# Two-layer graph network, head products: weights made stationary, two pairs of graphs moving in one product, and the transposed sums turned back by block moves

## Chip, cores and metric

One NeuronCore of a Trainium2 chip runs the kernel, in float32 throughout. The metric is device time in microseconds (us) of one launch, the median of several runs; lower is better. The engines are named as in the profile: PE (TensorE matmul), PEld (its weight load), DVE (VectorE), ACT (ScalarE), POOL (GpSimd) and SP (SyncE, which here issues every DMA; its queue is written SPq).

## The reference

Inputs are 128 graphs of 128 nodes with 256 features, and their weighted adjacency matrices. Both layers are residual with a layer norm and a relu ahead:

```python
h = relu(layernorm(x));  x = x + (adj @ (h @ w0) + b0)                  # layer 0
h = relu(layernorm(x))                                                  # layer 1, h is "feats"
feat = (h @ fc_w + fc_b) -> 8 heads of 256
q = feat @ q_w + q_b;  k = feat @ k_w + k_b                             # one number a node and head
attn = softmax(leaky_relu(q + k.T + (1 - adj) * -1e9, 0.01))            # 8 heads of 128 x 128 a graph
x = x + sigmoid((attn @ feat over heads) @ fp_w + fp_b + h)
```

The kernel multiplies attention by h first, and by one 256 x 256 matrix a head afterwards (fc_w of the head times fp_w of the head, made once in the setup).

## The kernel before

The work is done in 32 groups of 4 graphs (`GB = 4`), in a software pipeline that is written out by hand: `manual_schedule` keeps every engine's instructions in the program's order. While the head products of group g run, the attention of group g+1, the second norm of g+2, and the first layer of g+3 are worked on, and g+4 is loaded.

**The head products.** For each graph the 128 x 256 features h2 are split into two halves of 128 features, and the two graphs of a pair (b = 0, 1) with the two halves (c = 0, 1) make a 2 x 2 block matrix. It is multiplied with the head's 2 x 2 blocks of weights by a scheme of seven products instead of eight (`wt[0]` to `wt[6]`, sums of the weights' blocks made in `setup_sums`; `f[0]` to `f[6]`, sums of the aggregated features made in `take`). A unit is one pair of graphs and one half of the 8 heads, so a group has 4 units. In `aggregate` (L592) the features are stationary and the turned attention of 4 heads (512 columns) moves, which gives the transposed aggregated features `g_ps` in PSUM, four a unit. `take` (L608) makes f0 to f6 of them: three ACT copies, two DVE sums that read PSUM, and two POOL differences (f5 in `five`, L603, and f2). In `multiply` (L636) f is stationary and 128 columns of weights move; the products of unit n-1 run while unit n is aggregated, in the order of `ORDER`:

```python
ORDER = [("g", 0, 0), 3, 0, ("g", 1, 1), 1, 4, ("g", 1, 0), 6, 5, ("g", 0, 1), 2]
```

These are 11 slots a unit and 44 a group. Seven sums over 8 heads gather in two PSUM banks (`acc0`, `acc1`), of the form nodes x features. `combine` (L654) adds them on DVE into z, in two steps (after product 4 and after product 2), once for each pair. `residual_a` (L683, POOL) has added the output bias to h2 before, `residual_b` (L687, POOL) adds h2 to z; `sigmoid` (a tanh on ACT), `finish` (DVE) and `store` follow.

**PSUM.** `ps_m` has 6 banks for everything short-lived, `ps_o` one for each of acc0 and acc1.

**The turn of the attention.** Softmax leaves attn as query x key; `aggregate` needs key x query. `move` (L558) exchanges 32 x 32 blocks between partitions with 16 DMAs a pair of graphs (`attnB`), `turn` (L570) turns the inside of the blocks with one DVE stream transpose a graph. h2 takes the same way (`move_h2` L431, 16 DMAs, and `turn_h2_blocks`). All these are issued by SP.

**What sets the order.** `PLAN` (L714) lists steps as (slot, group ahead, function, arguments); `FIRST_PLAN` and `SECOND_PLAN` are for groups 0 and 1. The steps that issue DMAs, in the order in which SP runs them in a group g: slot 3 `move_h2` of g+2 (16), slot 8 `begin` of g+4 (2) and `load_blocks` of g+3 (4), slot 18 the first 8 blocks of `move` for pair 0 of g+1, slot 28 k_mem of `turn_qk` (1) and the other 8 blocks, slot 30 six blocks of pair 1, slot 34 `load_k` (4), ten blocks of pair 1 and `store` of g-1 (1). That is 60 DMAs a group. `turn` stands at slot 34 for both graphs of pair 0 (for the group to come), and at slots 12 and 13 of the group itself for the two graphs of pair 1, whose first use is the aggregation at slot 22.

At slot 3 ACT's `take(0, 1, 1)` is followed by `n2_apply` of g+2, which writes the h2 that `move_h2` moves; ahead of it on ACT stands `leaky` of the first graph (slot 0), which waits for DVE's `masked` (slot 0: `spread`, a stream transpose, L508, and the mask's sum, L516).

Of the kernel before, what the change touches and what calls it, by code (L numbers as in the profile page):

```python
# [15 lines left out]
P = 128  # L16
# [12 lines left out]
def gnn_then_gat_kernel(  # L29
# [33 lines left out]
    ps_m = ctx.enter_context(tc.tile_pool(name="ps_m", bufs=6, space=PSUM))  # L63
    ps_o = ctx.enter_context(tc.tile_pool(name="ps_o", bufs=1, space=PSUM))
# [24 lines left out]
    fpb_j = const.tile([P, D], FP, name="fpb_j")  # L89

# [11 lines left out]
    sp = setup.enter_context(tc.tile_pool(name="setup", bufs=1))  # L110
    turning = ExitStack()
    tp_ = turning.enter_context(tc.tile_pool(name="turning", bufs=1, side="right"))
    NK = HD // P
    ROWS = NK + 2 * NC
# [4 lines left out]
    nc.sync.dma_start(rows_in[NK + NC : ROWS], k_w.rearrange("(c p) o -> c (p o)", p=P))  # L119
# [6 lines left out]
    def more_loads():  # L126
        nc.sync.dma_start(fpw, fp_w.rearrange("(k p) o -> p k o", p=P))
        nc.sync.dma_start(qkb[:, 0:1], q_b.partition_broadcast(P))
        nc.sync.dma_start(qkb[:, 1:2], k_b.partition_broadcast(P))
        for c in range(NC):  # L130
            nc.sync.dma_start(
                fpb_j.rearrange("p (j c q) -> p c j q", c=NC, q=Q)[:, c],
                fp_b.rearrange("(c j q) -> c j q", j=NB, q=Q)[c].partition_broadcast(P),
            )
# [15 lines left out]
    def setup_rows():  # L150

        cp = ps_m.tile([P, ROWS], FP, name="cp", tag="m")
# [3 lines left out]
            qkc[:, :, 0:2], cols[:, NK:ROWS].rearrange("p (two c) -> p c two", two=2)  # L156
# [21 lines left out]
    def setup_turn(c, both=True):  # L178

        for k4 in range(NK // 4):  # L180
            tp = ps_m.tile([P, 4, P], FP, name="tp", tag="m")
            for kk in range(4):
                nc.tensor.transpose(tp[:, kk, :], fcw[:, c, ts(4 * k4 + kk, P)], ident)
            copy = nc.vector.tensor_copy if both and k4 % 2 else nc.scalar.copy
            copy(
                fcwT[:, ts(k4, 4)].rearrange("p k (j c q) -> p k j c q", c=NC, q=Q)[:, :, :, c],
                tp.rearrange("p k (j q) -> p k j q", q=Q),
            )

    def setup_wqk():  # L190


        wp = ps_m.tile([P, 2, D], FP, name="wp", tag="m")
# [12 lines left out]
    def setup_wqk_turn():  # L206

        tp = ps_m.tile([P, 2, NC, P], FP, name="wt_ps", tag="m")
# [15 lines left out]
    def setup_weights(h, c, on_dve):  # L224

        to = (slice(0, 5, 4), slice(1, 3))
        mp = ps_m.tile([P, D], FP, name="mp", tag="m")
# [11 lines left out]
    def setup_bias():  # L239

        bp = ps_m.tile([P, 1], FP, name="bp", tag="m")
# [28 lines left out]
    def setup_fpb():  # L270

        bp = ps_m.tile([P, D], FP, name="fb_ps", tag="m")
        nc.tensor.matmul(bp, lhsT=ones, rhs=fb, start=True, stop=False)
        nc.tensor.matmul(bp, lhsT=ones, rhs=fb2[:, 0], start=False, stop=True)
        nc.vector.tensor_tensor(
            fpb_j.rearrange("p (j c q) -> p c j q", c=NC, q=Q),
            bp.rearrange("p (c j q) -> p c j q", j=NB, q=Q),
            fpb_j.rearrange("p (j c q) -> p c j q", c=NC, q=Q),
            ALU.add,
        )  # L280
# [81 lines left out]
    def turn_adj(s):  # L362
        tp = ps_m.tile([P, GB, P], FP, name="adj_ps", tag="m")
# [5 lines left out]
    def first_a(s, b2):  # L369
# [3 lines left out]
        pp = ps_m.tile([P, 2, NC, P], FP, name="ah_ps", tag="m")  # L373
# [12 lines left out]
    def first_b(s, b2):  # L386
# [3 lines left out]
        op = ps_m.tile([P, 2, D], FP, name="x1_ps", tag="m")  # L390
# [54 lines left out]
    def turn_h2(s, b2):  # L445
        if b2 == 0:
            s["h2T"] = gp.tile([P, GB, NC, P], FP, name="h2T", tag="h2T", bufs=1)
        tp = ps_m.tile([P, 2, NC, P], FP, name="h2T_ps", tag="m")
# [9 lines left out]
    def make_qk(s, w=wqk):  # L458

        qk = ps_m.tile([P, P], FP, name="qk_ps", tag="m")  # L460
# [12 lines left out]
    def turn_qk(s):  # L473


        tp = ps_m.tile([P, GB, Q], FP, name="q_ps", tag="m")
# [93 lines left out]
    def turn(s, b):  # L570

        aT = s["aT", b] = pool["attnT"].tile([P, H, P], FP, name="attnT", tag="attnT")
        nc.vector.transpose(  # L573
            aT.rearrange("p h (i r) -> p i h r", r=Q), s["ab", b // 2][:, :, b % 2]
        )

    def turn_by_products(s, b):

        aT = s["aT", b] = pool["attnT"].tile([P, H, P], FP, name="attnT", tag="attnT")
        for h4 in range(2):  # L580
            tp = ps_m.tile([P, 4, P], FP, name="aT_ps", tag="m")
            for h in range(4):
                n = H * (b % 2) + 4 * h4 + h
                nc.tensor.transpose(tp[:, h, :], s["a", b // 2][:, ts(n, P)], ident)
            copy = nc.vector.tensor_copy if h4 else nc.scalar.copy
            copy(aT[:, ts(h4, 4)], tp)

    HU = H // 2  # L590

    def aggregate(u, b, c):  # L592
        s, pair, half = u["s"], u["pair"], u["half"]
        u["g", b, c] = ps_m.tile([P, HU, P], FP, name="g_ps", tag="m")
        nc.tensor.matmul(  # L595
            u["g", b, c],
            lhsT=s["h2"][:, 2 * pair + b].rearrange("p j c q -> p (j c q)")[:, ts(c, P)],
            rhs=s["aT", 2 * pair + b][:, ts(half, HU), :],
            start=True,
            stop=True,  # L600
        )

    def five(u):  # L603
        f = u["f"]
        f[5] = pool["un"].tile([P, HU, P], FP, name="f5", tag="f5")
        nc.gpsimd.tensor_tensor(f[5], f[4], f[0], ALU.subtract)  # L606

    def take(u, b, c, with_five=True):  # L608
# [3 lines left out]
        def new(m):  # L612
            f[m] = pool["un"].tile([P, HU, P], FP, name=f"f{m}", tag=f"f{m}")
# [6 lines left out]
        elif (b, c) == (1, 0):  # L620
            nc.vector.tensor_tensor(new(4), g, f[3], ALU.add)  # L621
            nc.vector.tensor_tensor(new(6), f[0], g, ALU.subtract)
            if with_five:
                five(u)
# [7 lines left out]
    ORDER = [("g", 0, 0), 3, 0, ("g", 1, 1), 1, 4, ("g", 1, 0), 6, 5, ("g", 0, 1), 2]  # L632
    FIRST = (3, 6)
    LAST = (4, 2)

    def multiply(u, m):  # L636

        half = u["half"]
        bank, slot = SLOT[m]
        if half == 0 and m in FIRST:  # L640
            u["s"]["acc", u["pair"], bank] = ps_o.tile(
                [P, 4, P], FP, name=f"acc{bank}", tag=f"acc{bank}"
            )
        acc = u["s"]["acc", u["pair"], bank]
        for h in range(HU):
            nc.tensor.matmul(  # L646
                acc[:, slot, :],
                lhsT=u["f"][m][:, h, :],
                rhs=wt[m][:, half * HU + h, :],
                start=(half == 0 and h == 0 and m in FIRST),  # L650
                stop=(half == 1 and h == HU - 1 and m in LAST),
            )

    def combine(u, m):  # L654
# [3 lines left out]
        s, pair = u["s"], u["pair"]  # L658
        z = s["z"][:, ts(pair, 2), :].rearrange("p b (h o) -> p (b h) o", o=P)
# [4 lines left out]
        def both(t):  # L664
            return t.unsqueeze(1).to_broadcast([P, 2, P])

        acc = s["acc", pair, m == 2]
        if m == 4:
            p1 = small.tile([P, P], FP, name="p1", tag="p1", bufs=2)
            w = s["w"] = small.tile([P, 2, P], FP, name="w", tag="w", bufs=2)  # L670
            nc.vector.tensor_copy(p1, acc[:, 0])
            add(w, acc[:, 1:3], both(p1))
            add(z[:, 0], acc[:, 3], p1)
        elif m == 2:
            w = s["w"]
            p6 = small.tile([P, P], FP, name="p6", tag="p6", bufs=2)
            v = small.tile([P, 2, P], FP, name="v", tag="v", bufs=2)
            nc.vector.tensor_copy(p6, acc[:, 0])
            add(v, acc[:, 1:3], both(p6))
            add(z[:, 2:4], w, both(v[:, 0]))  # L680
            add(z[:, 1], w[:, 1], v[:, 1])

    def residual_a(s, pair):  # L683
        h = s["h2"][:, ts(pair, 2)].rearrange("p b j c q -> p b (j c q)")
        nc.gpsimd.tensor_tensor(h, h, fpb_j.unsqueeze(1).to_broadcast([P, 2, D]), ALU.add)  # L685

    def residual_b(s, pair):  # L687
# [16 lines left out]
    def store(s, b0, nb):  # L704
# [22 lines left out]
        (7, "u", take, 0, 1, 0),  # L727
# [6 lines left out]
        (11, -1, residual_b, 1),  # L734
        (11, "u", take, 1, 0, 0),
        (11, 1, leaky, 2),
        (12, 0, turn, 2),
        (12, 1, masked, 3),
        (12, 1, normal, 0),
        (13, 0, turn, 3),  # L740
# [3 lines left out]
        (17, "u", take, 1, 1, 0),  # L744
# [7 lines left out]
        (21, 0, residual_a, 0),  # L752
# [9 lines left out]
        (28, "u", take, 2, 1, 0),  # L762
# [9 lines left out]
        (30, 1, move, 1, range(6)),  # L772
        (31, "u", take, 2, 0, 1),
        (32, "u", combine, 1, 2),
        (32, 0, residual_b, 0),
        (33, "u", take, 3, 0, 0),
        (34, 2, load_k),
        (34, 1, move, 1, range(6, 16)),
        (34, -1, store, 0, GB),
        (34, 1, turn, 0),  # L780
        (34, 1, turn, 1),
# [6 lines left out]
        (39, "u", take, 3, 1, 0),  # L788
# [5 lines left out]
        (43, 0, residual_a, 1),  # L794
# [8 lines left out]
        (7, "u", take, 0, 1, 0, False),  # L803
# [3 lines left out]
        (7, "u", five, 0),  # L807
# [12 lines left out]
        (17, "u", take, 1, 1, 0),  # L820
# [8 lines left out]
        (21, 0, residual_a, 0),  # L829
# [20 lines left out]
        (28, "u", take, 2, 1, 0),  # L850
# [12 lines left out]
        (32, 0, residual_b, 0),  # L863
# [15 lines left out]
        (38, 1, turn, 0),  # L879
        (38, 1, normal, 3),  # L880
        (39, "u", take, 3, 1, 0),
        (39, 3, first_b, 0),
        (39, 3, n2_stats, 0),
        (39, 1, turn, 1),
# [7 lines left out]
        (43, 0, residual_a, 1),  # L892
# [5 lines left out]
    plans = {0: FIRST_PLAN, 1: SECOND_PLAN}  # L898
# [109 lines left out]
    setup_sums(1)  # L1008
    setup.close()
    pool["un"] = ctx.enter_context(tc.tile_pool(name="unit", bufs=2))  # L1010
    units = [None]
    for g in range(NG):
        cur = groups[g]
        cur["z"] = pool["un"].tile([P, GB, D], FP, name="z", tag="z")
        last = units[-1]
        units = [{"s": cur, "pair": i // 2, "half": i % 2, "f": {}} for i in range(4)]
        for slot in range(4 * len(ORDER)):
# [6 lines left out]
            for at_, who, f, *args in plans.get(g, PLAN):  # L1024
                if at_ != slot:
                    continue
                if who == "u":
                    u = last if args[0] < 0 else units[args[0]]
                    if u:
# [76 lines left out]
```

## Time and profile before

| | |
|---|---|
| median of 3 runs | 1513.42 us (1512.85 to 1514.95) |
| profiled execution | span 1512.1 us from first to last instruction, 1.3 us below the median; no other time is recorded for this execution |
| mean granted TensorE clock | 0.996 |
| busy | PE 98%, PEld 79%, DVE 85%, ACT 73%, POOL 66% |
| group period in the middle of the run | 44.89 us (first aggregation of one group to that of the next, the same within 1 ns over groups 2 to 27) |
| first aggregation of groups 0, 1, 2 | at 60.39, 119.36 and 166.78 us |
| first aggregation of groups 28 to 31 | at 1333.86, 1378.81, 1418.46 and 1461.58 us; the last instruction ends at 1512.1 |
| DMAs | 253752 packets, 139.18 MB, the 16 DMA engines 40.5% busy with SP's queue |

A group line of the page reads: line, engine, operation, written<-read tile, shape and count, then busy time and mean duration of one in ns, then the engine's idle time just ahead of it with what ended it. A timeline line reads: start in us, length in us, engine, line, operation, and how many of them are merged. Matmuls are pipelined, so their pace is the distance from start to start and not their duration. A float32 matmul of the program shows as two matmuls. SP has no busy time on the page, since issuing a DMA is not counted as busy: its load is read from the timeline.

### The profile page before, as it was taken

How to read it: one execution, taken by the hardware profiler on the slowest of the kernel's cores; microseconds unless marked ns; L12 is line 12 of the kernel's file. 1: busy time of each engine (PE TensorE's matmuls, PEld its weight loads, DVE VectorE, ACT ScalarE, POOL GpSimd, SP SyncE). 2: the span in 40 equal slices, each digit the busy share in tenths (PEclk: the TensorE clock that was granted, in tenths of full speed). 3: DMA queues.
4: the chain of work that ended last, by engine and by line, in shares of the span. 5: the costliest groups of instructions: out<-in, count | busy, mean ns of one | idle time of the engine just before them, and what ended most of it. 6: DMA issues, size and time to landing. Idle time of an engine off the chain costs nothing.

```text
span 1512.1 us, 30658 instructions
## 1 busy us (share of the span) xinstructions
PE 1478.6 (98%) x9969; PEld 1198.0 (79%) x9969; DVE 1288.5 (85%) x2150; ACT 1103.5 (73%) x3847; POOL 1004.6 (66%) x879
## 2 busy tenths in 40 slices
PE   7889999999999999999999999999999999999998
PEld 5667888887888888888888888888788888888787
DVE  5778988888998888898888898888899888888753
ACT  4888777788777788777778777778877778876641
POOL 5666677676667767667767667767666776766563
PEclk9999999999999999999999999999999999999999
DMA  6124444444434444434444444444443444433320
GB/s 190 31 50 84 98 88 105 92 102 95 97 86 105 97 98 99 97 84 103 108 89 98 95 101 86 106 94 98 96 99 85 106 96 98 97 77 81 73 71 28
DMA packets 253752, 139.18 MB, mean 92 GB/s; under 512 B 169988, under 2 KB 221592, under 8 KB 253336
## 3 DMA queue, kind: packets, MB, share of 16 engines
q1 hardware_dynamic: 253592, 137.23, 40.5%
q8 instruction: 78, 1.28, 0.4%
q14 instruction: 82, 0.67, 0.2%
HBM read 39.60 MB, written 17.30 MB: 38 GB/s over the span
## 4 chain that ended last, share of the span: by engine, by line
PE 91%; DVE 3%; ACT 2%; POOL 1%; SPq 1%; DMA 1%; issue 1%; DVEq 0%; POOLq 0%
PE acc L646 51%; PE g_ps L595 28%; PE x_ps L393 7%; PE ah_ps L377 4%; PE qk_ps L463 1%; ACT attn L545 1%; ACT attn L529 1%; SPq L436 1%; ACT h L329 1%; DVE st L296 0%; DVE attn L508 0%; DVE attn L516 0%; DMA rows_in<-in_L_gnn_k_w_dram 0%; POOL attn L554 0%; DVE nmax L537 0%
## 5 line engine op out<-in xcount | busy, mean ns | idle before, releaser
L646 PEld LDWEIGHTS acc<-wts,f 128*128 128x128 f32 x7168 | 889.0, 192 | 244.7 <-issue 202.0
L646 PE MATMUL acc<-wts,f 128*128 128x128 f32 x7168 | 894.5, 275 | 4.6 <-DVE z L662 2.5
L595 PE MATMUL g_ps<-attnT,h 128*128 128x512 f32 x1024 | 527.1, 597 | 0.0
L545 ACT ACTIVATE attn<-attn,nmax 128x128 f32<-128x128 f32 x1024 | 398.1, 401 | 1.0 <-DVE nmax L537 1.0
L606 POOL TENSOR_TENSOR f<-f,f 128x512 f32<-128x512 f32 x128 | 164.1, 1282 | 268.2 <-DVE f L621 268.2
L529 ACT ACTIVATE attn<-attn,q 128x128 f32<-128x128 f32 x1024 | 313.5, 395 | 18.6 <-DVE attn L516 15.4
L554 POOL TENSOR_TENSOR attn<-attn,total 128x1024 f32<-128x1024 f32 x128 | 245.0, 1914 | 99.0 <-DVE total L553 93.7
L626 ACT COPY f<-g_ps 128x512 f32<-128x512 f32 x128 | 74.0, 578 | 262.4 <-PE g_ps L595 262.4
L545 ACT ACTIVATION_READ_ACCUMULATOR attn<-attn,nmax 128x1 f32 x1024 | 204.8, 200 | 0.0
L627 POOL TENSOR_TENSOR f<-f,f 128x512 f32<-128x512 f32 x128 | 192.4, 1503 | 9.6 <-ACT f L626 6.9
L516 DVE TENSOR_TENSOR attn<-attn,mask 128x1024 f32<-128x1024 f32 x128 | 179.8, 1405 | 4.5
L537 DVE TENSOR_REDUCE nmax<-attn 128x8 f32<-128x1024 f32 x128 | 153.9, 1203 | 17.4 <-ACT attn L529 17.3
L595 PEld LDWEIGHTS g_ps<-attnT,h 128*128 128x128 f32 x1024 | 156.0, 192 | 7.7 <-issue 6.7
L508 DVE STREAM_TRANSPOSE attn<-kq 128x1024 f32<-128x1024 f32 x128 | 157.0, 1227 | 5.3 <-DMA kq<-k_mem 5.3
L573 DVE STREAM_TRANSPOSE attnT<-attnB 128x1024 f32<-128x1024 f32 x124 | 148.6, 1217 | 11.4 <-issue 6.2
L393 PE MATMUL x_ps<-w_sb,ahT 128*128 128x256 f32 x512 | 120.8, 380 | 0.9 <-ACT ahT L384 0.9
L621 DVE TENSOR_TENSOR f<-g_ps,f 128x512 f32<-128x512 f32 x128 | 87.0, 680 | 37.0 <-ACT f L619 32.7
L690 POOL TENSOR_TENSOR z<-z,h 128x256 f32<-128x256 f32 x126 | 89.2, 729 | 34.9 <-DVE z L662 29.8
L685 POOL TENSOR_TENSOR h<-h,fpb_j 128x512 f32<-128x512 f32 x64 | 109.8, 1715 | 0.1
L617 ACT COPY f<-g_ps 128x512 f32<-128x512 f32 x128 | 74.5, 582 | 41.0 <-PE g_ps L595 41.0
L393 PEld LDWEIGHTS x_ps<-w_sb,ahT 128*128 128x128 f32 x512 | 92.7, 191 | 11.8 <-ACT ahT L384 1.8
L700 DVE SCALAR_TENSOR_TENSOR z<-z,x 128x1024 f32<-128x1024 f32 (+2 forms) x34 | 89.2, 2627 | 6.0 <-ACT z L696 6.0
(110 smaller groups left out, 1314.6 us busy)
## 6 DMA issues: line engine op xcount, KB each, us to landing
attnB<-attn SPq DMA_DIRECT2D x992, 64.0 KB, 2.0
xg<-in_x_dram SPq DMA_DIRECT2D x32, 512.0 KB, 4.1
out_dram<-z SPq DMA_DIRECT2D x31, 512.0 KB, 3.1
h2B<-h SPq DMA_DIRECT2D x464, 32.0 KB, 1.9
ag<-in_adj_dram SPq DMA_DIRECT2D x32, 256.0 KB, 4.6
agB<-in_adj_dram SPq DMA_DIRECT2D x116, 64.0 KB, 4.4
fcw<-in_L_gnn_fc_w_dram SPq DMA_DIRECT2D x2, 1024.0 KB, 8.2
fpw<-in_L_gnn_fp_w_dram SPq DMA_DIRECT2D x1, 2048.0 KB, 14.5
```

Source lines behind the costliest of these rows:

```text
L393: nc.tensor.matmul(op[:, bb, :], lhsT=s["ahT"][:, 2 * b2 + bb, c, :], rhs=w0_sb[:, c, :], start=(c == 0), stop=(c == NC - 1),)
L508: nc.vector.transpose(s["v", b], s["kq"][:, :, b].unsqueeze(3).to_broadcast([P, NB, H, Q]),)
L516: nc.vector.tensor_tensor(a, a, s["mask"][:, b, :] .rearrange("p (j c) -> p j c", c=Q) .unsqueeze(2) .to_broadcast([P, NB, H, Q]), ALU.add,)
L529: nc.scalar.activation(a[:, :, h, :], a[:, :, h, :], AF.Prelu, bias=s["q"][:, b, h : h + 1], alpha=0.01,)
L537: nc.vector.tensor_reduce(nmax, a.rearrange("p j h c -> p h j c"), AX.XY, ALU.max, negate=True)
L545: nc.scalar.activation(a[:, :, h, :], a[:, :, h, :], AF.Exp, bias=s["nmax", b][:, h : h + 1], accum_out=s["total", b][:, h : h + 1],)
L554: nc.gpsimd.tensor_tensor(a, a, total.unsqueeze(1).unsqueeze(3).to_broadcast([P, NB, H, Q]), ALU.mult)
L573: nc.vector.transpose(aT.rearrange("p h (i r) -> p i h r", r=Q), s["ab", b // 2][:, :, b % 2])
L595: nc.tensor.matmul(u["g", b, c], lhsT=s["h2"][:, 2 * pair + b].rearrange("p j c q -> p (j c q)")[:, ts(c, P)], rhs=s["aT", 2 * pair + b][: ...
L606: nc.gpsimd.tensor_tensor(f[5], f[4], f[0], ALU.subtract)
L627: nc.gpsimd.tensor_tensor(new(2), f[1], f[5], ALU.subtract)
L646: nc.tensor.matmul(acc[:, slot, :], lhsT=u["f"][m][:, h, :], rhs=wt[m][:, half * HU + h, :], start=(half == 0 and h == 0 and m in FIRST), ...
```

## The change

1. **Products.** `multiply` now takes the weights as stationary operand and moves f. Where a unit held one pair and 4 heads, in groups 2 to 30 it holds both pairs and 2 heads, so 256 columns (two pairs of 128 nodes) move at once, and half as many matmuls are issued. Groups 0, 1 and 31 (`PAIRWISE`) keep one pair a unit and 128 columns. The sums come out transposed, features x nodes, and acc0 and acc1 take two PSUM banks each; `ps_m` goes from 6 to 4 banks (during the setup a second pool `ps_s` lends 2 more).
2. **Summed halves.** `sum_features` (POOL, once a group) adds the two feature halves of every second graph; `aggregate(1, 2)` uses it in the place of (1, 0). `take` copies f4 (ACT), makes f5 on DVE from PSUM and f6 and f2 on POOL; one DVE operation over PSUM a unit goes, one ACT copy comes. `aggregate` issues two matmuls of 256 columns where it issued one of 512.
3. **Attention tiles.** They are kept by pair and half of the heads; `turn` makes both graphs of a pair for 4 heads. In groups 2 to 30 unit 0 needs both pairs' first halves, so `turn(1, 0)` stands at slot 40 of the group before, the second halves at slots 12 and 13.
4. **Way back.** `combine` runs once a group over both pairs and writes `zT`; the output bias is added on ACT (two operations) instead of `residual_a` on POOL. `move_z`, at slot 11, exchanges the blocks of zT with 16 DMAs issued by SP, each 32 partitions of 1 KB; `turn_z`, at slot 20, is one DVE stream transpose; then `residual` on POOL for four graphs. Group 31 turns zT with PE transposes (`turn_z_by_products`).
5. **Setup.** The output bias becomes a column (`fpb_o`), loaded with the other rows.

```diff
-    ps_m = ctx.enter_context(tc.tile_pool(name="ps_m", bufs=6, space=PSUM))
-    ps_o = ctx.enter_context(tc.tile_pool(name="ps_o", bufs=1, space=PSUM))
+    ps_m = ctx.enter_context(tc.tile_pool(name="ps_m", bufs=4, space=PSUM))
...
+    def turn(s, pair, half):
         nc.vector.transpose(
+            attention_tile(s, pair, half).rearrange("p b h (i r) -> p i b h r", r=Q),
+            s["ab", pair][:, :, :, ts(half, HU)],
         )
...
+        for n, pair in enumerate(u["pairs"]):
...
+            nc.tensor.matmul(
+                g[:, n * w : (n + 1) * w],
+                lhsT=lhsT,
+                rhs=s["aT", pair, u["half"]][:, b, u["heads"]],
...
+        elif (b, c) == (1, 2):
+            nc.scalar.copy(new(4), g)
+            nc.vector.tensor_tensor(new(5), g, f[0], ALU.subtract)
+            nc.gpsimd.tensor_tensor(new(6), f[3], f[5], ALU.subtract)
...
             nc.tensor.matmul(
-                acc[:, slot, :],
-                lhsT=u["f"][m][:, h, :],
-                rhs=wt[m][:, half * HU + h, :],
+                acc,
+                lhsT=wt[m][:, u["half"] * HU + h, :],
+                rhs=f[:, n],
...
+    def move_z(s):
+        s["zB"] = pool["un"].tile([P, NB, GB * NC * Q], FP, name="zB", tag="zB", bufs=1)
+        for i in range(NB):
+            for j in range(NB):
+                nc.sync.dma_start(s["zB"][ts(i, Q), j], s["zT"][ts(j, Q), ts(i, D)])
+    def turn_z(s):
+        s["z"] = pool["un"].tile([P, GB, D], FP, name="z", tag="z", bufs=1)
+        nc.vector.transpose(
+            s["z"].rearrange("p (a b) (c j q) -> p j (b c) a q", b=2, j=NB, q=Q),
+            s["zB"].rearrange("p j (k a q) -> p j k a q", a=2, q=Q),
+        )
...
-        (11, -1, residual_b, 1),
+        (11, -1, move_z),
-        (12, 0, turn, 2),
+        (12, 0, turn, 0, 1),
-        (13, 0, turn, 3),
+        (13, 0, turn, 1, 1),
-        (21, 0, residual_a, 0),
+        (20, -1, turn_z),
+        (21, -1, residual, 0),
+        (21, -1, residual, 1),
+        (30, 1, sum_features),
+        (32, 1, move, 1, range(6, 16)),
         (34, 2, load_k),
-        (34, 1, move, 1, range(6, 16)),
-        (34, 1, turn, 0),
-        (34, 1, turn, 1),
+        (34, 1, turn, 0, 0),
+        (40, 1, turn, 1, 0),
-        (43, 0, residual_a, 1),
```

## The prediction

> **What bounds the kernel now.** I read the page first (busy shares and the costliest groups), then the timeline of PE in the middle of the run, then that of SP, which the page gives no share, then those of DVE and ACT at the start of a group.
>
> ```profile
> PE 1478.6 (98%) x9969; PEld 1198.0 (79%) x9969; DVE 1288.5 (85%) x2150; ACT 1103.5 (73%) x3847; POOL 1004.6 (66%) x879
> ...
> attnB<-attn SPq DMA_DIRECT2D x992, 64.0 KB, 2.0
> ...
> h2B<-h SPq DMA_DIRECT2D x464, 32.0 KB, 1.9
> ```
>
> PE has no room: in the middle every group takes 44.89 us, to the ns. Its pace by form is read from start to start (columns: start, length, engine, line, operation, how many):
>
> ```profile
> 701.06 1.89 PE L393 MATMUL x_ps<-w_sb,ahT 128*128 128x256 f32 x8
> 702.79 1.05 PE L646 MATMUL acc<-wts,f 128*128 128x128 f32 x8
> ...
> 706.29 1.95 PE L646 MATMUL acc<-wts,f 128*128 128x128 f32 x16
> 708.08 1.02 PE L595 MATMUL g_ps<-attnT,h 128*128 128x512 f32 x2
> 708.94 1.95 PE L646 MATMUL acc<-wts,f 128*128 128x128 f32 x16
> ```
>
> 128 columns: (708.08-706.29)/16 = 0.112 us a matmul; 256 columns, with a new weight each: (702.79-701.06)/8 = 0.216; 512: 0.86/2 = 0.430. The weight loads hide at all three. So 224 product matmuls x 0.112 + 32 x 0.430 = 38.8 of the 44.9 us.
>
> SP is the other engine that I look at, since the change gives it 16 more DMAs a group. One period of its queue:
>
> ```profile
> 708.17 0.53 SPq L706 DMA_DIRECT2D out_dram<-z  x1
> 712.34 11.49 SPq L436 DMA_DIRECT2D h2B<-h  x16
> 723.95 0.51 SPq L68 DMA_DIRECT2D xg<-in_x_dram  x1
> 724.56 0.45 SPq L70 DMA_DIRECT2D ag<-in_adj_dram  x1
> 725.07 3.15 SPq L78 DMA_DIRECT2D agB<-in_adj_dram  x4
> 729.04 5.00 SPq L565 DMA_DIRECT2D attnB<-attn  x8
> 734.48 0.36 SPq L483 DMA_DIRECT2D k_mem<-k  x1
> 734.88 9.68 SPq L565 DMA_DIRECT2D attnB<-attn  x14
> 744.60 2.04 SPq L488 DMA_DIRECT2D kq<-k_mem  x4
> 746.69 6.21 SPq L565 DMA_DIRECT2D attnB<-attn  x10
> 753.00 0.53 SPq L706 DMA_DIRECT2D out_dram<-z  x1
> ```
>
> The reader is to see that SP is nearly full too. A DMA holds it for about 0.59 us (L565: median 0.589 of 992, minimum 0.507; L436: 0.599), with 0.04 between two, whether it carries 32 or 64 KB. It idles only where data are late: 708.70 to 712.34 (h2 of n2_apply), 728.22 to 729.04 and 734.04 to 734.48, 4.9 us of 44.8. The last blocks of pair 1 are issued at 752.9, 2.6 us into the next group (which starts at 750.32), and land some 1.4 us later; nobody minds, as `turn` of that pair stands at slot 12.
>
> **The change part by part.**
>
> *Products.* In 29 groups 112 matmuls of 0.216 replace 224 of 0.112: 25.09 - 24.19 = 0.90 us. Aggregation: 64 x 0.216 - 32 x 0.430 = +0.06. PE's own work falls by 0.83 us a group, to 44.1; 29 x 0.83 = 24 us if PE stays the bound. The row L393 has the new form, so I take 0.216; by the trace's spread this is not the open question. The Trainium skill (TensorE: Matmul & The Clock Gate, Back-to-back issue gap) gives a warm matmul a fixed 2.5 ns beyond its columns. By that two matmuls saved into one would give back 2.5 ns and not 8, and the sum of this part would be 8 us.
>
> *Sums and their way to z.* DVE: four sums over PSUM of 0.68 go (-2.7 us a group); combine falls from 2 x 2.6 us to about 3.3 to 4.2 (the same columns in half the instructions; rows of 256 columns cost 0.42, of 512 0.68); `turn_z` adds 1.22 (row L573). ACT gets 4 copies of 0.58 and two bias additions of 0.4, +3.1 us (73% to about 80%). POOL loses 2 x 1.72 and gains a sum of about 0.7. None of these is full, so they cost nothing as long as each stays hidden under PE; uncovered, the ACT part would be 3.1 us a group.
>
> *Four banks in the place of six.* From the trace I compared, for each short-lived PSUM tile, its first matmul with the end of the last reader of the tile four before it: the tightest pair has 0.8 us to spare (q_ps behind the third unit's first g_ps), the next 1.9. ACT's added copies can eat this: 0 to 1 us a group. I take 0.
>
> *Setup and end.* Setup changes by tenths of a us, either way. At the end four PE transposes (4 x 0.11 and 0.29 to finish) and two sums of 0.42 enter behind the last sums: +1.3 us.
>
> *16 DMAs on SP.* move_z is partition to partition, 32 rows, as L565 and L436 are; by them it costs 16 x 0.633 = 10.1 us of SP a group. Bounds: the fastest steady row (kq, 0.48 from start to start) gives 7.6, the mean of L436 with its slow ones (0.68) 10.8; nothing in the trace is near zero. I take 10.1, as L565 is nearest. SP works 44.8 - 4.9 = 39.9 us in the period shown and 38.4 in the next, so the 16 make 49 to 50, above PE's 44.1. Here the Trainium skill speaks against me: DMA: Bandwidth & Descriptors (Issuing engines are not separate DMA queues) says that the sequencer's time to start a DMA is usually small beside the DMA itself, and its table for the GpSimd path puts the dispatch at about 50 ns. By that, 16 would cost 0.8 us and the whole would end near 1491. The row of this case, 0.589 of 992, decides.
>
> *What queues behind it.* SP runs in order, so h2B, attnB and z share one line, and its end has become a deadline: `turn(1, 0)` at slot 40 needs all 16 blocks of pair 1 before PE can start the next group. So a loop closes. Call the end of turn(1, 0) T:
>
> - T to the first h2B. DVE goes on with the sum L400, norm statistics, spread and mask, then ACT with leaky, take and n2_apply; only then may SP go on. In the trace of before the same steps, back to back, go from 747.88 (L400 starts) to 757.23 (h2B starts): 9.35 us.
>
> ```profile
> 752.31 2.45 ACT L529 ACTIVATE attn<-attn,q 128x128 f32<-128x128 f32 x8 [0.29 <-DMA attnB<-attn]
> 754.67 0.56 ACT L619 COPY f<-g_ps 128x512 f32<-128x512 f32 x1
> 755.13 2.07 ACT L329 ACTIVATE h<-x,nb,rstd 128x256 f32<-128x256 f32 x4
> ```
>
> - SP without a pause: h2B to agB 15.1 (15.9 and 14.3 in two periods), z 10.1, eight attnB 5.05, k_mem 0.4, twenty-four attnB 15.6: 46.3. load_k and store now come behind and fall into SP's wait.
> - The last DMA lands 2.0 after its start, 1.4 after SP is done with it; turn 1.22 and 0.1 to start.
>
> 9.4 + 46.3 + 1.4 + 1.3 = **58.4 us a group** against 44.9. On the way, `turn_z` at slot 20 waits until about T+36 for z's blocks, and holds DVE, the second norm's q and k (so PE, at slot 28), the residuals and two `normal`s on POOL with it; by the rows they are done at about T+46, when SP asks for pair 1, and PE still gets through its last 16 slots (16 us) by T+55. So they are late, but inside the loop.
>
> **Sum**, against the profiled span of 1512.1. Group 0 starts at 60.4 as before, group 1 59.0 later; group 1: 58.4 - 2.7 (it doesn't start behind such a turn) = 55.7; groups 2 to 27: 26 x 58.4 = 1518.4; group 28 without `begin`: 57.3; group 29 without loads: 54.3; group 30 without h2B is PE's again: 44; group 31 and the end: 50.6 + 1.3 = 51.9. Together 1901; with the 1.3 us that the median lies above the span, **1902 us**.
>
> **Rivals.**
>
> - *SP's throughput alone* (0.13). If the loop doesn't close (h2B comes before SP asks for it), a period is SP's issuing time, 38.4 to 39.9 + 10.1, so 49.3: (49.3-44.9) x 28 = +124, **1637**. For it: h2 depends on x1 alone. Against it: n2_apply stands on ACT behind leaky and take, and these behind DVE and PE.
> - *PE's gain stands* (0.08), the side faster than before: SP issues z's DMAs in its idle time. Price: -24 + 1.3, **1491**. It decides from the pace of SP's queue: pair 1 must land by slot 40 (T+40.8), and from h2B's start at 6.9 after the group's to the last landing there are 70 DMAs: (40.8-6.9-2.0)/70 = 0.45 us each. L565 holds 0.63; only kq's 0.48 comes near.
> - *PE's gain is eaten* (0.05): SP keeps up, but ACT's 3.1 us and the four banks hold PE by 1 to 2 us a group, less the 0.83 saved: up to +35, **1530**.
> - *No difference* (0.02): the gain and the new waits cancel.
>
> The first case has 0.72. Its own bounds: z at kq's pace 55.9 a group, 1832; SP at the means with its slow DMAs (0.66) and 1 to 2 us of late data 61.5, 1990. With SP's throughput alone taken in, the range is 1630 to 1990. Faster by over 0.2%: 0.08; within 0.2%, about what a measurement of this kernel can tell from no change: 0.02; slower: 0.90.
>
> **What would show it.** In the profile after: a period near 58 us; PE busy near 76%; SP's timeline without gaps from h2B to the last attnB, with 16 rows zB<-zT of 0.59; DVE's turn waiting for attnB and turn_z for zB, several us a group each, where before all of L573's waits for attnB made 5.2 us in the whole run; products of 256 columns at 0.216. I am wrong if z's DMAs take far less than 0.5 us of SP, if attnB's do where many wait, or if PE idles for PSUM banks or ACT and not for a turn.

## The result

The changed kernel takes **1950.4 us** (median; 1948.6 to 1952.0), against 1514.2 us for the kernel before, run beside it on the same chip: 1.288 times as long, 95% interval 1.286 to 1.289. The profiled execution took 1952.0 us, 1.8 above its span of 1950.2. The forecast was 1902 with a range of 1630 to 1990: slower, by the mechanism named, 2.5% short.

### The profile page after: what moved, and what is told of

The parts are those of the page before. It is cut to its first block, busy times and chain, and to the rows that moved or that the text cites. A ratio compares the mean times of both kernels' runs of the same rounds, so it can differ in the third digit from the quotient of the medians.

```text
span 1950.2 us, 26524 instructions
## 1 busy us (share of the span) xinstructions
PE 1584.1 (81%) x7661; PEld 1330.7 (68%) x7661; DVE 1184.3 (61%) x1816; ACT 1204.3 (62%) x4045; POOL 915.3 (47%) x845
## 3 DMA queue, kind: packets, MB, share of 16 engines
q1 hardware_dynamic: 276348, 153.38, 31.8%
## 4 chain that ended last, share of the span: by engine, by line
SPq 35%; DVE 20%; issue 12%; ACT 11%; POOL 10%; DMA 6%; PE 5%; DVEq 0%; POOLq 0%; ACTq 0%
SPq L562 18%; SPq L727 10%; ACT attn L526 7%; SPq L433 5%; POOL attn L551 5%; DVE attnT L575 3%; DVE attn L513 3%; DVE attn L505 3%; PE acc L663 3%; POOL z L760 2%; DMA kq<-k_mem 2%; ACT h L326 2%; DVE st L293 2%; DMA attnB<-attn 2%; DVE zT L691 2%
## 5 line engine op out<-in xcount | busy, mean ns | idle before, releaser
L663 PE MATMUL acc<-f,wts 128*128 128x256 f32 (+1 forms) x3920 | 952.8, 387 | 85.5 <-DVE zT L691 85.5
L663 PEld LDWEIGHTS acc<-f,wts 128*128 128x128 f32 x3920 | 753.7, 206 | 217.9 <-ACT f L636 93.2
L611 PE MATMUL g_ps<-attnT,h 128*128 128x256 f32 (+1 forms) x1464 | 428.8, 413 | 38.3 <-DVE attnT L575 35.5
L611 PEld LDWEIGHTS g_ps<-attnT,h 128*128 128x128 f32 x1464 | 287.7, 203 | 98.3 <-DVE attnT L575 43.8
L575 DVE STREAM_TRANSPOSE attnT<-attnB 128x1024 f32<-128x1024 f32 x124 | 152.3, 1229 | 255.7 <-DMA attnB<-attn 151.7
L542 ACT ACTIVATION_READ_ACCUMULATOR attn<-attn,nmax 128x1 f32 x1024 | 209.1, 204 | 0.0
L731 DVE STREAM_TRANSPOSE z<-zB 128x1024 f32<-128x1024 f32 x31 | 38.6, 1245 | 251.8 <-DMA zB<-zT 251.8
L474 PE MATMUL q_ps<-ident,qk 128*128 128x128 f32 x32 | 13.9, 435 | 206.3 <-DVE total L550 201.0
L636 ACT COPY f<-g_ps 128x512 f32<-128x512 f32 x128 | 75.2, 588 | 166.4 <-PE g_ps L611 165.3
L505 DVE STREAM_TRANSPOSE attn<-kq 128x1024 f32<-128x1024 f32 x128 | 157.0, 1226 | 3.3 <-DMA kq<-k_mem 3.3
L474 PEld LDWEIGHTS q_ps<-ident,qk 128*128 128x128 f32 x32 | 5.7, 178 | 218.2 <-issue 181.4
L628 ACT COPY f<-g_ps 128x512 f32<-128x512 f32 x128 | 74.6, 582 | 117.4 <-PE g_ps L611 117.3
L632 ACT COPY f<-g_ps 128x512 f32<-128x512 f32 x128 | 74.5, 582 | 115.8 <-PE g_ps L611 115.7
L611 PE MATMUL g_ps<-attnT,hs 128*128 128x256 f32 (+1 forms) x488 | 132.5, 392 | 9.0 <-POOL hs L599 9.0
```

Of the source, the lines that this page charges most:

```text
L505: nc.vector.transpose(s["v", b], s["kq"][:, :, b].unsqueeze(3).to_broadcast([P, NB, H, Q]),)
L542: nc.scalar.activation(a[:, :, h, :], a[:, :, h, :], AF.Exp, bias=s["nmax", b][:, h : h + 1], accum_out=s["total", b][:, h : h + 1],)
L575: nc.vector.transpose(attention_tile(s, pair, half).rearrange("p b h (i r) -> p i b h r", r=Q), s["ab", pair][:, :, :, ts(half, HU)],)
L611: nc.tensor.matmul(g[:, n * w : (n + 1) * w], lhsT=lhsT, rhs=s["aT", pair, u["half"]][:, b, u["heads"]], start=True, stop=True,)
L663: nc.tensor.matmul(acc, lhsT=wt[m][:, u["half"] * HU + h, :], rhs=f[:, n], start=(first and n == 0 and m in ((3, 6) if each else (3, 1, 6, ...
```

## The profile after

First the page of the changed kernel: the busy line, the chain that ended last, then three groups and one DMA issue.

```profile
PE 1584.1 (81%) x7661; PEld 1330.7 (68%) x7661; DVE 1184.3 (61%) x1816; ACT 1204.3 (62%) x4045; POOL 915.3 (47%) x845
...
SPq 35%; DVE 20%; issue 12%; ACT 11%; POOL 10%; DMA 6%; PE 5%; DVEq 0%; POOLq 0%; ACTq 0%
...
L575 DVE STREAM_TRANSPOSE attnT<-attnB 128x1024 f32<-128x1024 f32 x124 | 152.3, 1229 | 255.7 <-DMA attnB<-attn 151.7
...
L731 DVE STREAM_TRANSPOSE z<-zB 128x1024 f32<-128x1024 f32 x31 | 38.6, 1245 | 251.8 <-DMA zB<-zT 251.8
...
L474 PE MATMUL q_ps<-ident,qk 128*128 128x128 f32 x32 | 13.9, 435 | 206.3 <-DVE total L550 201.0
...
zB<-zT SPq DMA_DIRECT2D x496, 32.0 KB, 1.9
```

No engine is full any more. `turn` (L575) waits 256 us in the run, 152 of them put down to attnB and 100 to kq, which it doesn't read; `turn_z` (L731) waits 252 us for zB; and PE waits 206 us at the q and k of the second norm (L474), behind DVE, which `turn_z` holds. The chain says it in one row: SP's queue has the largest share. The same two rows before, the chain and `turn` (L573 there):

```profile
PE 91%; DVE 3%; ACT 2%; POOL 1%; SPq 1%; DMA 1%; issue 1%; DVEq 0%; POOLq 0%
L573 DVE STREAM_TRANSPOSE attnT<-attnB 128x1024 f32<-128x1024 f32 x124 | 148.6, 1217 | 11.4 <-issue 6.2 <-DMA attnB<-attn 5.2
```

One period of SP, from the h2 of one group to that of the next (columns: start, length, engine, line, operation, how many):

```profile
1031.25 11.66 SPq L433 DMA_DIRECT2D h2B<-h  x16
...
1044.15 3.11 SPq L77 DMA_DIRECT2D agB<-in_adj_dram  x4
1047.35 10.43 SPq L727 DMA_DIRECT2D zB<-zT  x16
1057.88 4.98 SPq L562 DMA_DIRECT2D attnB<-attn  x8
1062.96 0.53 SPq L480 DMA_DIRECT2D k_mem<-k  x1
1063.53 15.66 SPq L562 DMA_DIRECT2D attnB<-attn  x24
...
1091.31 10.94 SPq L433 DMA_DIRECT2D h2B<-h  x16
```

Left out are xg and ag, and behind the last attnB kq (1079.24) and the store (1081.36). From 1031.25 to 1079.19 there is no gap: 47.9 us, where the forecast had 46.3. From the last attnB to the next h2B pass 12.1 us (forecast 1.4 + 1.3 + 9.35 = 12.05). What fills these 12.1 us is read on DVE and ACT:

```profile
1080.83 1.25 DVE L575 STREAM_TRANSPOSE attnT<-attnB 128x1024 f32<-128x1024 f32 x1 [3.85 <-DMA kq<-k_mem]
```
```profile
1086.39 2.45 ACT L526 ACTIVATE attn<-attn,q 128x128 f32<-128x128 f32 x8 [2.94 <-DVE attn L513]
...
1089.21 2.08 ACT L326 ACTIVATE h<-x,nb,rstd 128x256 f32<-128x256 f32 x4
```

`turn(1, 0)` starts when the last blocks have landed (the wait is put down to kq, which the turn doesn't read; kq was issued just behind them), then come the sum, the statistics, the mask, leaky, take and n2_apply, and SP goes on at 1091.31. That is the closed loop of the forecast. The period, averaged over groups 2 to 27, is 59.67 us; before it was 44.89, and 26 x 14.8 = 384 of the 436 us lie there.

## The experiments

The theory: SP's line, from h2B through z to the last attnB, has become the path, because `turn(1, 0)` needs its end and n2_apply, its beginning, comes after that turn. Rivals: SP's throughput alone; the transfers of z and not their issue; four banks and ACT's added copies. "Period" is the mean of groups 2 to 27. The kernel before ran at 1513 to 1515 us beside each.

### e1: the loads into SP's wait

```diff
         (3, 2, n2_apply, 1),
+        (3, 4, begin),
+        (3, 3, load_blocks),
         (3, 2, move_h2),
...
-        (8, 4, begin),
-        (8, 3, load_blocks),
```

> Only the place of six DMAs on SP changes: begin and load_blocks are issued at slot 3 ahead of move_h2, where SP of the changed kernel sits idle for 10 us a group. Loop theory (T to h2B, SP's line, landing, turn(1,0)): the six take 4.1 to 4.3 us out of the loop, 59.7 - 4.2 = 55.5 us a group, about 1833 us in all. Rival 1 (SP's issuing time alone, 49.7 us of DMAs a group, or the bytes on the DMA engines): nothing changes, 1950. Rival 2 (four PSUM banks, ACT's added copies, PE's clock after its pauses): nothing changes, 1950.

Measured: 1849.1 us, 1.221 (1.218 to 1.223), period 55.7. The six loads hold SP for 4.2 us in the period above, and moved into its wait they give back 4.0 a group. Were the number of DMAs the limit, nothing would have come back. The loop stands; throughput alone is out.

### e2: h2 also earlier

```diff
         (0, "u", take, 0, 0, 0),
+        (0, 2, n2_apply, 0),
+        (0, 2, n2_apply, 1),
+        (0, 4, begin),
+        (0, 3, load_blocks),
+        (0, 2, move_h2),
...
-        (40, 1, turn, 1, 0),
         (40, 3, first_b, 1),
         (40, 3, n2_stats, 1),
+        (40, 1, turn, 1, 0),
```

> As the run before, and the other stretch of the loop is cut as well: n2_apply and the loads and move_h2 stand at slot 0 right behind the first take, and DVE makes the last x1 and its statistics ahead of turn(1,0) and not behind it. All 76 DMAs stay on SP. Loop theory: h2B starts about 4.2 us after the turn and not 12.1 after the last attnB; 4.2 + 11.3 (h2B) + 10.3 (z) + 20.5 (attnB) + 0.6 + 1.4 + 1.3 = 49.6 us a group, about 1667 us, and SP without a pause worth naming. Rival 1: 1950, as no DMA is taken away. Rival 2: 1950, as PE, ACT and PSUM have the same work.

Measured: 1778.5 us, 1.174 (1.171 to 1.177), period 53.0. Right in direction, half the size: SP then waits inside its line, ahead of k_mem (69.7 us in 28 groups, 2.5 each), which is most of the 3.4 us that are missing.

### e3: z by PE transposes, no DMAs for it

```diff
-        if s["g"] == NG - 1:
+        if True:
...
-        (11, -1, move_z),
...
-        (20, -1, turn_z),
-        (21, -1, residual, 0),
-        (21, -1, residual, 1),
+        (20, -1, turn_z_by_products, 0),
+        (21, -1, turn_z_by_products, 1),
```

> move_z and turn_z go; every group's transposed sums are turned back by eight PE transposes and added to h2 by DVE from PSUM, as the changed kernel does for its last group. SP has 60 DMAs a group again. Loop theory: 59.7 - 10.3 = 49.4 us a group, about 1650 us; still far above the kernel before, since the deadline of turn(1,0) and the loop stay. If the 16 DMAs were the whole cause (no loop), the period would be PE's, 44.1 + 0.9 = 45.0, about 1520 us. Rival 2: more pressure on four banks (two tiles more a group), 1950 or above.

Measured: 1831.4 us, 1.209 (1.206 to 1.212), period 55.4. The 16 DMAs are gone, 10.4 us of SP, and only 4.3 came back: the 49.4 expected from the loop alone was wrong, and so was PE's 45.0. SP of this kernel:

```profile
1037.79 2.98 SPq L77 DMA_DIRECT2D agB<-in_adj_dram  x4
1043.18 4.99 SPq L562 DMA_DIRECT2D attnB<-attn  x8
1052.37 0.36 SPq L480 DMA_DIRECT2D k_mem<-k  x1
1052.77 15.94 SPq L562 DMA_DIRECT2D attnB<-attn  x24
```

Where z stood are two holes: 1040.8 to 1043.2, until POOL's first `normal` is done, and 1048.2 to 1052.4, until DVE has made k. ACT, which has 11% of the chain that ended last in the changed kernel, has 45% of it here. The attention and the second norm had been nearly as late as z, beside it and hidden by it.

### e4 and e5: parts of the change made to the kernel before

e4 takes two PSUM banks from it; e5 gives it a deadline at the end of SP's line and nothing else: at slot 40 a small DVE copy that reads a column of each of pair 1's blocks, and the turn of pair 0's first graph behind it.

```diff
-    ps_m = ctx.enter_context(tc.tile_pool(name="ps_m", bufs=6, space=PSUM))
+    ps_m = ctx.enter_context(tc.tile_pool(name="ps_m", bufs=4, space=PSUM))
```
```diff
+    def touch(s):
+        seen = small.tile([P, NB], FP, name="seen", tag="seen")
+        nc.vector.tensor_copy(seen, s["ab", 1][:, :, 0, 0, 0])
...
-        (34, 1, turn, 0),
...
+        (40, 1, touch),
+        (40, 1, turn, 0),
```

> The kernel before with four short-lived PSUM banks and not six, nothing else. From the trace of before the tightest tile has 0.8 us to spare with four, so: 1513 to 1516 us (within 0.2%). Rival 2 (four banks hold PE): 1 to 2 us a group, 1540 to 1575.

> The kernel before with the deadline alone: at slot 40 DVE reads four columns of attnB of the next group's pair 1 (so it waits for all 16 blocks) and only then turns the first graph of pair 0, which PE needs at slot 0. Products, sums, PSUM and the 60 DMAs stay as before. Loop theory: 9.4 + 11.2 (h2B) + 4.3 (loads) + 5.0 + 0.4 + 9.2 + 2.1 (load_k) + 6.3 + 1.4 + 1.5, and up to 4 us of waits for normal and k_mem as the run e3 shows them, so 51 to 55 us a group, 1690 to 1800 us. If the 16 added DMAs were the cause and the deadline cost nothing: 44.9, 1515.

Measured: e4 1517.9 us, 1.002 (1.001 to 1.003). Four banks cost about 3 us in all there (1 to 5 by the interval), 2 us above the expected range; the period is 45.02 for 44.89. e5 1756.9 us, 1.160 (1.158 to 1.161), period 52.8: the order alone costs 7.9 us a group, with the same 60 DMAs and the kernel's old products. Its SP:

```profile
806.32 0.53 SPq L710 DMA_DIRECT2D out_dram<-z  x1
818.39 11.26 SPq L436 DMA_DIRECT2D h2B<-h  x16
...
852.88 6.21 SPq L565 DMA_DIRECT2D attnB<-attn  x10
```

From the h2B at 818.39 to the end of attnB at 859.09 it takes 40.7 us, and from the last attnB (806.22) to that h2B 12.2: together 52.9. In the kernel before, the period shown in the prediction has 40.6 (712.34 to 752.90) and 4.3 (to the next h2B at 757.23): all that the order adds lies in the second stretch. It is the same loop, with z's DMAs left out.

### e6, e7, e9, e10: taking the deadline away

e6 lets every group use one pair a unit (`PAIRWISE`), so that pair 1 is wanted at slot 12 again, as before the change; z's DMAs stay. e7 is e6 with z by PE transposes, as in e3. e9 is e7, and e10 is e6, with `load_k` ahead of pair 1's blocks.

```diff
-    PAIRWISE = (0, 1, NG - 1)
+    PAIRWISE = range(NG)
...
-        (12, 0, turn, 0, 1),
+        (12, 0, turn, 1, 0),
...
-        (40, 1, turn, 1, 0),
+        (40, 1, turn, 0, 1),
...
```
```diff
+        (30, 2, load_k),
         (30, 1, move, 1, range(6)),
...
         (32, 1, move, 1, range(6, 16)),
-        (34, 2, load_k),
...
```

> The changed kernel with one pair and 128 columns in all groups (its own form of groups 0, 1 and 31): pair 1's turns stand at slots 12 and 13 again, so the deadline is gone; move_z and its 16 DMAs on SP stay. If SP's issuing time now paces: 49.7 us a group and a little for late data, 50 to 51, 1655 to 1685 us. If the deadline was all: PE's 45, about 1520.

> As the run before, and z is turned back by PE transposes, so neither the deadline nor the 16 DMAs: PE's 44.9 + 0.9 = 45.8 us a group, about 1545 us with the first and last groups' extra. If weights held still, the summed halves, the four banks or ACT's added copies cost by themselves, it is above that.

Measured: e6 1937.2 us, 1.279 (1.277 to 1.281), period 59.1; e7 1835.8 us, 1.212 (1.210 to 1.214), period 55.6. Both expectations failed: without that deadline the time hardly moved. What DVE waits for in e7 (columns: who, for whom, us in total, times, longest):

```profile
DVE attn L505 <- DMA kq<-k_mem: 176.4, 30, 9.2
```

The change had also put `load_k` behind all 24 attnB, where it had stood behind 14. `spread` (L505), at slot 0, reads kq, and n2_apply comes behind it. So the line's end was wanted twice, by `turn(1, 0)` and by kq, and to take away one left the other.

> As e7 (one pair a unit, z by PE transposes, 60 DMAs), and load_k stands ahead of pair 1's blocks and not behind them. In e7 DVE's spread waited for kq (176 us in all): the change had put load_k at the end of SP's line too, so the same loop closed through kq. If that is what held e7 at 55.6 us a group, the period now falls to PE's 45 to 47, 1530 to 1580 us. If stationary weights, summed halves, four banks or ACT's copies hold it, it stays near 55, 1830.

> As e9, but z goes back by the 16 block moves on SP and turn_z (so e6 with load_k ahead of pair 1's blocks): no deadline on the last blocks, 76 DMAs. In e9 SP is at work for 40.8 of 49.3 us and waits 8.5 (3.3 for h2, 5.2 for normal and k_mem). z's 10.3 us fill the 5.2 first. If SP's issuing time paces: 51.1 us, and up to 3.3 more if h2 stays late, so 51 to 54.5 a group, 1690 to 1800 us. If the 16 DMAs cost nothing without the deadline: 48 to 50, 1650 or less.

Measured: e9 1648.8 us, 1.090 (1.087 to 1.092), period 49.2, 6.4 less than e7; the fall is there, but not down to the 45 to 47 expected. e10 1843.4 us, 1.218 (1.215 to 1.221), period 56.2, above the 51 to 54.5 expected. In e10 nothing at the end of the line is late; it is the middle that is, on DVE and then on PE:

```profile
DVE z L731 <- DMA zB<-zT: 264.1, 31, 10.2
```
```profile
PE q_ps L474 <- DVE total L550: 237.0, 29, 9.6
```

The DMAs of z make `turn_z` late, that holds DVE, and PE loses it at L474. The expectation had only SP's time in its sum. The four periods side by side, from one pair of causes:

| period, us | z by 16 DMAs on SP | z by PE transposes |
|---|---|---|
| line's end wanted at once | 59.7 (changed kernel) | 55.4 (e3) |
| not wanted (pairwise, kq early) | 56.2 (e10) | 49.2 (e9) |

Either cause alone costs 6 to 7 us a group, both together 10.4: they overlap. The two rows also differ in the form of the products, 256 columns or 128; with the line's end still wanted, through kq, that form changed the period by -0.6 (e6 against the changed kernel) and +0.2 (e7 against e3). e9 is still 4.3 above the kernel before; by my estimate 0.9 of it is PE's own transposes (eight matmuls of 128 columns at 0.112); the rest shows as small waits of PE, the largest of them for `combine` before it may write acc again (30.8 us in the run).

### e8: the first sum of halves ahead of the setup's sums

```diff
     leaky(s0, 2)
+    sum_features(s0)
     setup_sums(0)
...
     setup_sums(1)
-    sum_features(s0)
```

> The changed kernel with the first group's sum_features ahead of the sums of weights on POOL, and nothing else: group 0's period falls from 67.1 to about 60 us, the rest stays: 1950 - 7 = 1943 us. If something else delays group 0, 1950.

Measured: 1954.2 us, 1.290 (1.288 to 1.292). Group 0's period fell from 67.1 to 61.2, near the 60 expected, but the first aggregation came 2.2 us later. Of the gain of 3.3 left by group 2, 1.3 are gone by group 28 and the other 2.0 in group 30, the last group is 1.3 longer, and the total didn't fall. Why is open.

### e11: z's DMAs issued by POOL

```diff
-                nc.sync.dma_start(s["zB"][ts(i, Q), j], s["zT"][ts(j, Q), ts(i, D)])
+                nc.gpsimd.dma_start(s["zB"][ts(i, Q), j], s["zT"][ts(j, Q), ts(i, D)])
```

> The changed kernel with z's 16 DMAs issued by POOL's queue and not by SP's: the same bytes on the same 16 DMA engines. If the issuing on SP is what they cost: about e3's 55.4 us a group, 1830 us (a little more if POOL's own issuing holds up normal). If the transfers are what costs: 59.7, 1950. If POOL takes well over 1 us a DMA, its normals come late and the period goes above 60.

Measured: 1887.1 us, 1.248 (1.245 to 1.250), period 57.0. The same bytes move; taken off SP's line they cost less, so part of z's price is the issuing. Only 2.7 came back. POOL now issues them, and its `normal`s, for which SP waits, stand behind (14 of the 16 hold POOL from 1061.56 on for 6.98 us). SP's wait for the `normal`s, 31.9 us in the changed kernel, is here:

```profile
SPq L562 <- POOL attn L551: 284.5, 32, 27.8
```

### c1: a version that might beat both

It keeps 256 columns, sends z and h2 through HBM with 13 DMAs in the place of 32 (57 a group), and does most of the attention's steps 4 to 8 slots earlier. Its core:

```diff
+        for j in range(NB):
+            nc.sync.dma_start(s["hb"][ts(j, Q)].rearrange("p i b c q -> p i (b c q)"), h[j])
...
+        nc.sync.dma_start(s["z_mem"], s["zT"])
...
+            nc.sync.dma_start(s["zB"][ts(i, Q)], z[i])
...
+        (0, 2, n2_apply, 0),
+        (0, 2, n2_apply, 1),
+        (0, 2, h2_out),
```

> The changed kernel (two pairs, 256 columns) with short lines on SP and early data: z and h2 go through HBM (z 1 DMA out and 4 back, h2 4 out and 4 back, so 57 DMAs a group in the place of 76), n2_apply and the loads stand at slot 0, load_k ahead of the last blocks of pair 1, and the attention of the next group is begun 5 to 8 slots earlier, so that pair 1's blocks can be issued by about T+38. Loop theory: nothing on SP is later than PE any more, so PE's 44.1 us a group, 1485 to 1515 us. If the deadline still binds by a few us, 46 to 50 a group, 1550 to 1660. If 256 columns, four banks or ACT's copies held the changed kernel, it stays above 55 a group, 1830 or more.

Measured: 1759.2 us, 1.162 (1.159 to 1.165), period 52.7, between the bands expected for a deadline (46 to 50) and for the other causes (above 55). SP's line is short here and SP idles, for zT, for n2_apply and for the normals:

```profile
SPq L730 <- DVE zT L697: 206.2, 31, 21.6
SPq L431 <- ACT h L326: 198.8, 28, 7.6
SPq L568 <- POOL attn L557: 135.8, 32, 15.9
```

So fewer DMAs are not enough. `turn` hardly waits any more (16.4 us in the run, 7.0 of them for attnB); DVE waits 174.2 us for zB at `turn_z`, PE waits 104.4 us behind DVE's turns, and DVE has the largest share of the chain, 27%. Which of them sets the 52.7 was not tested. No version tried beats the kernel before.

## Why the prediction was right, and where it was off

**The mechanism** was right. The loop is in the trace, with its two stretches within 1.6 and 0.1 us of the forecast in the period shown (1.2 and 0.1 over 25 periods), and e1 (the loads) and e5 (the order alone) move it as it says. The pace of z's DMAs was right (10.43 for 16; taken 10.1), and so was the way in which `turn_z` holds DVE and PE's q and k. Products of 256 columns went at 0.216 us. Four banks at nothing were right to 0.2% (e4, at the old products).

**The terms of the sum**, forecast and measured:

| | forecast | measured | difference |
|---|---|---|---|
| to the first aggregation | 60.4 | 61.7 | +1.3 |
| group 0 | 59.0 | 67.1 | +8.1 |
| group 1 | 55.7 | 57.9 | +2.2 |
| groups 2 to 27 | 26 x 58.4 | 26 x 59.67 | +33 |
| groups 28, 29, 30 | 57.3, 54.3, 44 | 57.8, 47.4, 47.4 | -2.9 |
| group 31 and the end | 51.9 | 59.3 | +7.4 |

The sum of the differences is the 49 us between 1901 and the span of 1950.2. Two thirds is the middle: SP's stretch takes 47.5 us on the mean of 25 periods (47.9 in the one shown) and not 46.3. h2B to agB is 15.1, as forecast (the 16.1 of the period shown is the longest), z is 10.4 for 10.1, and the attnB with k_mem are 22.0 for 21.05. That the groups 28 to 30 come out near is in part luck: group 29 is 6.9 below its forecast, group 30 3.4 above. The pace of kq, the forecast's lower bound for z, was read too low: its DMAs start 0.50 us apart (median; 0.54 on the mean), not 0.48. Group 0 is a step that I passed over ("Setup changes by tenths of a us"): the first sum of halves stands behind `setup_sums` on POOL, and PE waits for it:

```profile
70.00 2.08 PE L611 MATMUL g_ps<-attnT,hs 128*128 128x512 f32 x2 [6.38 <-POOL hs L599]
```

e8 confirms that wait as group 0's, though not as a gain for the whole. In the last group I added work only behind the last sums ("+1.3 us"), while the attention blocks of group 31 came late behind z on SP:

```profile
1901.02 2.37 DVE L575 STREAM_TRANSPOSE attnT<-attnB 128x1024 f32<-128x1024 f32 x2 [10.98 <-DMA attnB<-attn]
```

**What the forecast had too simple**, though its number held: it had one chain, and 10.1 of its 13.5 us a group were z's DMAs, as if without them the period would fall by as much. e3 gives 4.3. Beside z's stretch ran the attention's own chain, only some 4 us a group earlier, and beside `turn(1, 0)` a second reader of the line's end: load_k, of which the forecast said only that it falls into SP's wait. That is true of SP and not of kq's reader.

**The rivals.** SP's throughput alone (1637) fell: SP idles about 10 us a group. "PE's gain stands" (1491) needed 0.45 us a DMA; measured was 0.65. "PE's gain is eaten" had ACT and the banks; e4 leaves 3 us for the banks (with the old products), and the small waits left in e9, some 3.4 us a group, look like its kind, visible only once SP is out of the way; ACT has 43% of e9's chain. The transfers as such don't fill the DMA engines: SP's queue keeps them 31.8% busy, 40.5% before. Open are this rest, which I have not taken apart, what holds c1, and why e8's gain was lost.

## What to carry to other kernels

Before a change adds DMAs to a queue that runs in order, multiply them by the measured issue time (here about 0.6 us, for 32 and for 64 KB) and ask who reads the last one in the line, for a reader that wants it at once can cost as much as the DMAs (e5: 7.9 us a group without one DMA added). When the new path is found, look for its neighbours, the readers and chains that are almost as late: what you take off the path comes back only as far as the next of them (e3: 4.3 of 10.4). A saving on the full engine (0.8 us a group here, by the forecast) is worth nothing once another queue carries the period.

## What the runs showed of the hardware

**PE runs at half clock after a pause.** In the changed kernel, behind the wait at L474:

```profile
1111.45 1.89 PE L663 MATMUL acc<-f,wts 128*128 128x256 f32 x8
...
1120.21 0.45 PE L474 MATMUL q_ps<-ident,qk 128*128 128x128 f32 x1 [6.01 <-DVE total L550]
1120.45 3.62 PE L663 MATMUL acc<-f,wts 128*128 128x256 f32 x8
```

The eight products behind it go at 0.43 us each, those ahead of it at 0.216; the granted clock is 0.50 from 1120 to 1125 us, 1.00 again from 1126, and 0.913 over the run (0.996 before; 0.993 in e9, where PE's waits are short). So PE shows busy for 81% of the span, where the forecast had 76%. The Trainium skill (TensorE: Matmul & The Clock Gate, Part 1) states half rate after an idle window of about 3.4 us and full rate after at least as long a busy one; this trace agrees, with a pause of 6.0 us and full rate 5 to 6 us after its end. What the half clock costs here no run isolates; PE has 5% of the chain that ended last.

**A DMA issued by POOL** of the same 32 rows of 1 KB held POOL for 0.50 us and landed 3.6 us after its issue (e11); issued by SP it took 0.65 from start to start and landed after 1.9.
